# The feed forward's left operands: made by rows and transposed by DMA, with the shift moved into the bias

## The chip, the cores and the metric

The kernel runs on one core of a Trainium2 chip. The metric is the device time of one execution in microseconds (us); lower is better. The engines named below are PE (matmul), PEld (its weight load, which overlaps PE), DVE (vector), ACT (scalar), POOL, and SP, which here only issues DMAs. All DMAs of one core share 16 DMA engines.

## The reference, cut to what matters

The reference is one transformer-like block with modulation (adaLN): a long convolution in place of attention, then a linear layer with a low-rank update in place of the feed forward. The input `x` is 4 x 1024 x 2048 in float32.

```python
mod = (silu(c) @ wmod).reshape(4, 6, 1, -1)
sa, ca, ga, sb, cb, gb = (mod[:, i] for i in range(6))
ga, gb = (sign(g) * max(abs(g), 0.25) for g in (ga, gb))
h = layernorm(x) * (1 + ca) + sa
x = x + ga * (causal_conv(h, K) + D[0] * h)        # K, 2048 taps, comes from the S4 parameters
h = layernorm(x) * (1 + cb) + sb                   # second modulation
out = h @ W.T + bias + sum_e coeffs[e] * scales[e] * (h @ A[e].T) @ Bf[e].T
return x + gb * out
```

The last two lines are the feed forward. The low-rank update is linear in `h`, so the kernel adds it to `W.T` once (it calls the sum the merged weight) and the feed forward is one product of 4096 rows by 2048 by 2048.

## The kernel before

**Convolution part.** 32 row tiles `r` of 128 rows go through `conv_prep` (normalise, transpose by PE, scale and shift, split into two float16 halves), `conv_mm` (a Toeplitz product on PE) and `conv_post` (the result goes to the DRAM array `x1d`, with the statistics for the second layer norm in `ln2`). Between the matmuls of a row tile there are ten ticks; the table `PLAN` says what is emitted in each. "S" is one step of the generator `rest`, which spreads other work over the rows: `prep_lora` (low-rank factors), `section` (one of the six modulation vectors from `wmod`, 16 loads of 1 MB and 64 matmuls each), and `merge`, eight times, which makes the merged weight for two blocks of 128 inner positions, scales each inner position by a power of two (`winv` is the inverse), and writes the weight operands to the DRAM array `wcd`. Every `MR` steps of the merge there is one step of a section. `fold_scale` at the end of `rest` folds `winv` and a common power of two into the modulation's columns `cb` (scale) and `sb` (shift).

**Feed forward part.** The output is cut in 16 units `u` of 256 rows, done twice, for two halves `q` of the columns. Each 256 x 2048 by 2048 x 1024 product is made by Strassen's scheme with seven products instead of eight. Operand `i` of the seven is a 1024 x 128 left tile in two float16 halves (`hl`, "lf" in the profile) and a weight `w` of 1024 x 512 in two halves. `ffn_unit` runs the seven products in the order `ORDER = (0, 4, 5, 1, 6, 2, 3)`, 24 matmuls each (line 750 of the profile), and combines them through `copy` (ACT, line 758) and `finish` (DVE, lines 773 and 774). After each product there is a tick.

**The left operands.** `left` makes the seven left tiles of a unit. It loads the unit's two row tiles from `x1d` and normalises them on ACT (line 690), transposes 16 blocks of 128 columns of both on PE (line 700, tile `tp`, 32 transposes a unit), scales and shifts each block on ACT, because channels now lie on partitions (line 702, tile `gt`), forms sums on DVE (lines 719 to 726), and `put` splits each into halves on ACT and DVE (lines 712 and 713). In the first pass, `q` = 0, these tiles are used straight from SBUF; `put` also writes them to the DRAM array `lfd`. In the second pass, `left_load` reads them back with a plain DMA (line 733). In the first pass the tick of `ffn_unit` emits parts of the next unit's `left` by the table `LPLAN`: four ticks of a unit carry eight PE transposes each. The left tiles of unit 0 are made in the convolution's last two rows.

**Queues.** Nearly all DMAs are issued by SP, in one order: weight loads (line 989), residual loads `xo` (line 767), output stores (line 775), `lfd` stores (line 714), `x1d` loads (line 689). An issue that has to wait holds back those behind it.

Of the kernel before, what the change touches and what calls it, by code (L numbers as in the profile page):

```python
# [12 lines left out]
F32 = mybir.dt.float32  # L13
# [11 lines left out]
P = 128  # L25
# [9 lines left out]
class Net:  # L35
# [302 lines left out]
    def mod_gate(self, pool, name, bias=None):  # L338
# [10 lines left out]
        if bias is not None:  # L349
            bt = pool.tile([P, 512], F32, tag="mg2", name="mg2")  # L350
            for q in range(4):
                nc.sync.dma_start(out=bt[32 * q : 32 * q + 32], in_=bias[ds(512 * q, 512)].partition_broadcast(32))
            v.tensor_tensor(bt, bt, g, MUL)
            outs.append(bt)
# [9 lines left out]
    def fold_scale(self, pool, mul, add, name, winv=None):  # L364
        v = self.nc.vector
        if winv is not None:
            for t in (mul, add):
                v.tensor_tensor(t, t, winv.unsqueeze(2).to_broadcast([P, NC, NB]), MUL)
        b = pool.tile([P, 2, NB], F32, tag="fsb", name="fsb")
        for i, t in enumerate((mul, add)):  # L370
            v.tensor_reduce(b[:, i, :], t.rearrange("p c b -> p b c"), AX.X, ALU.max, apply_absolute_value=True)
        m = pool.tile([P, NB], F32, tag="fsm", name="fsm")
        v.scalar_tensor_tensor(m, b[:, 0, :], LNMAX, b[:, 1, :], MUL, ADD)
        self.hs, inv = s, _ = self.pow2(self.cst, self.allmax(pool, m, NB, name), NB, name)
        for t in (mul, add):
# [91 lines left out]
    def merge(self, pool, tmp, c):  # L467
# [11 lines left out]
        for h in range(2):  # L479
            for q in range(4):  # L480
# [8 lines left out]
                yield  # L489

# [192 lines left out]
    def left(self, pl, u, res):  # L683
        nc, v = self.nc, self.nc.vector
        b = u // 4
        xs = []
# [8 lines left out]
        t = pl["t"].tile([P, NC, 2, P], F32, tag="t", name="gt")  # L695
        for c0 in range(0, NC, 2):
            tp = self.tps.tile([P, 2, 2, P], F32, tag="t", name="tp2")
            for c in range(2):
                for r in range(2):
                    nc.tensor.transpose(tp[:, c, r], xs[r][:, ds(P * (c0 + c), P)], self.ident)  # L700
            for c in range(2):
                nc.scalar.activation(  # L702
                    t[:, c0 + c], tp[:, c], AF.Identity,
                    bias=self.sb[:, c0 + c, b : b + 1], scale=self.cb[:, c0 + c, b : b + 1],
                )
            yield
        a11, a12 = t[:, 0:HC, 0, :], t[:, HC:NC, 0, :]
        a21, a22 = t[:, 0:HC, 1, :], t[:, HC:NC, 1, :]

        def put(i, s):  # L710
            hl = pl["l"].tile([P, HC, 2, P], F16, tag="l", name="lf")
            nc.scalar.copy(hl[:, :, 0, :], s)
            v.tensor_tensor(hl[:, :, 1, :], s, hl[:, :, 0, :], SUB)
            STQ(nc).dma_start(out=self.lfd[u, i], in_=hl)
            res[i] = hl

        put(0, a11)
        s = pl["s"].tile([P, HC, P], F32, tag="s", name="s")
        v.tensor_tensor(s, a21, a22, ADD)
        put(4, s)  # L720
        v.tensor_tensor(s, s, a11, SUB)
        put(5, s)
        put(1, a12)
        v.tensor_tensor(a21, a11, a21, SUB)
        put(6, a21)
        v.tensor_tensor(s, a12, s, SUB)
        put(2, s)
        put(3, a22)
        yield

    def left_load(self, pl, u, i):
        hl = pl["l"].tile([P, HC, 2, P], F16, tag="l", name="lf")
        self.nc.sync.dma_start(out=hl, in_=self.lfd[u, i])
        return hl

    def left_again(self, pl, u):
        return {i: self.left_load(pl, u, i) for i in ORDER}

    def ffn_unit(self, pl, u, q, lf, wc, tick):
# [3 lines left out]
        def prod(i, name):  # L743
# [4 lines left out]
            for k in range(HC):  # L748
                for x, y in ((0, 0), (0, 1), (1, 0)):
                    nc.tensor.matmul(  # L750
                        ps[name], lf[i][:, k, x, :], wc[i][k // 4][:, k % 4, y, :],
# [58 lines left out]
MR = 2  # L810
ACC, TPS = 5, 2
PLAN = ("PNSL", "NL", "NSL", "NTL", "SL", "SL", "SL", "SL", "FSL", "SSL")
LPLAN = ("LL", "LL", "LL", "LL", "L", "0", "")
# [19 lines left out]
def net(ctx: ExitStack, tc: tile.TileContext, io):  # L833
# [6 lines left out]
    k.lfd = k.dram.tile([NU, 7, P, HC, 2, P], F16, tag="lfd", name="lfd")  # L840
# [12 lines left out]
    def section(sec, pools):  # L853
# [5 lines left out]
        if sec == 0:  # L859
            k.sa = k.mod_column(msm, k.kpool, "sa", 0.0)  # L860
            k.hinv = k.fold_scale(msm, k.ca, k.sa, "fs1")
# [4 lines left out]
        elif sec == 4:  # L866
            k.cb = k.mod_column(msm, k.cst, "cb", 1.0)
        elif sec == 3:
            k.sb = k.mod_column(msm, k.cst, "sb", 0.0)
        else:  # L870
            _, k.gbd = k.mod_gate(msm, "gbd", io["bias"])
        yield

    def merges():
        yield from k.prep_lora(pl["lora"], pl["mrg"])
        for c in range(HC):
# [290 lines left out]
```

## Time and profile before

| | |
|---|---|
| time, median of 3 runs | 2144.5 us (2140.22 to 2147.28) |
| time of the profiled execution | 2141.87 us |
| span of the profiled execution | 2140.1 us |
| PE busy | 2082.4 us (97%) |
| DVE, ACT busy | 1308.4 us (61%), 923.7 us (43%) |
| moved by DMA | 484.11 MB, mean 226 GB/s |
| granted clock of PE, mean | 0.988 |

The span runs from the first to the last instruction of the program; the execution's own time is 1.8 us more. "Busy" is the union of an engine's instructions. In rows of groups the line is that of the code, the tile names follow, then the count, the busy time in us and the mean duration of one instruction in ns, then the idle time of the engine just before them and what ended it. The row of PEclk gives the clock granted to PE in tenths of full speed, and the row of DMA the mean busy share of the 16 DMA engines.

### The profile page before, as it was taken

The numbers are of one execution on the slowest core, as the hardware profiler recorded it, in microseconds if no ns is written. First come the engines' busy times: TensorE is split into PE (matmuls) and PEld (weight loads), VectorE is DVE, ScalarE is ACT, GpSimd is POOL, SyncE is SP. The second block draws the span as 40 slices with busy tenths as digits, with TensorE's granted clock in tenths as the row PEclk, the third lists the DMA queues.
The fourth block names the chain that finished last, engine by engine and source line by source line (L and its number), as shares of the span: only waits on it lengthen the run. The fifth ranks groups of instructions, "written<-read, shape, count | busy, mean of one in ns | idle before, by whom it ended". The sixth has DMA issues, their size and how long they took to land.

```text
span 2140.1 us, 28438 instructions
## 1 busy us (share of the span) xinstructions
PE 2082.4 (97%) x11113; PEld 1026.1 (48%) x11113; DVE 1308.4 (61%) x2353; ACT 923.7 (43%) x1695; POOL 6.3 (0%) x18
## 2 busy tenths in 40 slices
PE   7898999999999999999999999999999999999998
PEld 2344455555555555554545545555444444444444
DVE  5439898898979999665565565575533323332323
ACT  1325876677767777745454555555200000000000
POOL 0000000000000000000000000000000000000000
PEclk7999999999999999999999999999999999999999
DMA  9977566787776554387564564564794645454542
GB/s 401 373 307 278 225 227 265 285 310 262 276 278 227 187 192 173 139 346 258 190 241 180 202 240 179 203 235 172 283 341 163 192 151 167 164 170 165 177 157 69
DMA packets 127236, 484.11 MB, mean 226 GB/s; under 512 B 13608, under 2 KB 13768, under 8 KB 95998
## 3 DMA queue, kind: packets, MB, share of 16 engines
q1 hardware_dynamic: 126192, 477.55, 61.4%
q10 hardware_dynamic: 526, 2.63, 0.4%
q8 instruction: 87, 1.43, 0.3%
q0 software_dynamic: 384, 2.11, 0.2%
q14 instruction: 47, 0.39, 0.0%
HBM read 326.94 MB, written 155.30 MB: 225 GB/s over the span
## 4 chain that ended last, share of the span: by engine, by line
PE 67%; DVE 18%; ACT 6%; DMA 5%; issue 2%; SPq 0%; ACTq 0%; POOL 0%; DVEq 0%; POOLq 0%
PE fZ L750 22%; PE fY L750 15%; PE fX L750 15%; PE ya L614 5%; PE yb L614 3%; PE tp L700 3%; DVE wch L514 2%; PE modps L317 2%; DVE st L540 2%; DVE hc L593 2%; DVE y L641 2%; ACT x L660 2%; DMA wcd<-wch 1%; ACT t L582 1%; PE lps L486 1%
## 5 line engine op out<-in xcount | busy, mean ns | idle before, releaser
L750 PEld LDWEIGHTS <-lf 128*128 128x128 f16 x5376 | 526.0, 98 | 620.9 <-issue 1.4
L750 PE MATMUL fZ<-w,lf 128*128 128x512 f16 x2304 | 513.6, 379 | 0.8 <-ACT p L758 0.8
L750 PE MATMUL fX<-w,lf 128*128 128x512 f16 x1536 | 342.8, 379 | 0.0
L750 PE MATMUL fY<-w,lf 128*128 128x512 f16 x1536 | 342.0, 379 | 0.0
L614 PEld LDWEIGHTS <-hc 128*128 128x128 f16 x2304 | 215.3, 98 | 204.6 <-issue 41.6
L768 DVE TENSOR_TENSOR xo<-xo,gb 128x512 f32<-128x512 f32 x128 | 87.8, 690 | 238.7 <-DMA xo<-x1d 227.2
L582 ACT ACTIVATE t<-tp,sa,ca 128x128 f32<-128x128 f32 x480 | 188.1, 471 | 21.6 <-PE tp L578 12.9
L614 PE MATMUL ya<-kh,hs 128*128 128x512 f16 (+3 forms) x768 | 193.7, 326 | 3.7 <-DVE kh L284 2.6
L614 PE MATMUL ya<-kh,hc 128*128 128x512 f16 (+3 forms) x768 | 192.7, 328 | 3.8 <-ACT qs L627 3.6
L614 PE MATMUL yb<-kh,hc 128*128 128x512 f16 (+3 forms) x768 | 192.2, 327 | 1.8 <-DVE y L640 1.4
L758 ACT COPY p<-fZ 128x512 f32<-128x512 f32 x64 | 37.2, 581 | 286.8 <-PE fZ L750 272.1
L614 PEld LDWEIGHTS <-hs 128*128 128x128 f16 x1152 | 105.9, 98 | 108.6 <-issue 28.4
L758 ACT COPY p<-fX 128x512 f32<-128x512 f32 x32 | 18.7, 585 | 316.3 <-PE fX L750 210.4
L702 ACT ACTIVATE gt<-tp,sb,cb 128x256 f32<-128x256 f32 x256 | 124.9, 576 | 60.8 <-PE tp L700 60.8
L317 PE MATMUL modps<-wm,sct 128*32 128x512 f32 x768 | 118.8, 662 | 14.1 <-DMA wm<-in_wmod 14.1
L614 PE MATMUL ya<-kl,hc 128*128 128x512 f16 (+3 forms) x384 | 125.8, 328 | 0.0
L614 PE MATMUL ya<-kl,hs 128*128 128x512 f16 (+3 forms) x384 | 125.1, 326 | 0.7 <-DVE kl L285 0.7
L614 PE MATMUL yb<-kl,hc 128*128 128x512 f16 (+3 forms) x384 | 125.6, 327 | 0.0
L773 DVE TENSOR_TENSOR fin<-fX,gb 128x512 f32<-128x512 f32 x32 | 22.1, 692 | 128.4 <-PE fX L750 128.3
L593 DVE TENSOR_TENSOR hc<-t,hc 128x512 f16<-128x512 f32 x128 | 87.5, 684 | 6.6 <-ACT hc L592 6.4
L486 PE MATMUL lps<-lbh,lac 128*128 128x512 f16 x256 | 86.3, 379 | 1.2 <-DVE we L488 1.2
L578 PE MATMUL tp<-ident,n 128*128 128x128 f32 x512 | 79.3, 280 | 8.1 <-ACT t L582 6.3
(264 smaller groups left out, 2228.0 us busy)
## 6 DMA issues: line engine op xcount, KB each, us to landing
wm<-in_wmod SPq DMA_DIRECT2D x96, 1024.0 KB
lfd<-lf SPq DMA_DIRECT2D x112, 512.0 KB
lf<-lfd SPq DMA_DIRECT2D x112, 512.0 KB
x<-in_x SPq DMA_DIRECT2D x32, 1024.0 KB
x1d<-y SPq DMA_DIRECT2D x32, 1024.0 KB
x<-x1d SPq DMA_DIRECT2D x32, 1024.0 KB
xo<-x1d SPq DMA_DIRECT2D x128, 256.0 KB
out<-xo SPq DMA_DIRECT2D x128, 256.0 KB
```

The source lines that it names most:

```text
L317: self.last = self.nc.tensor.matmul(self.modps[32 * g : 32 * g + 32, :], self.sct[:, j].rearrange("p r b -> p (r b)"), w[:, ds(512 * g, 512)],
L486: nc.tensor.matmul(ps, la[:, x, k, h], y[:, k, osl], start=(n == 0), stop=(n == 5))
L514: v.tensor_tensor(hl[:, :, 1, :], tv, hl[:, :, 0, :], SUB)
L578: nc.tensor.transpose(tp[:, k], n[:, ds(P * (c0 + k), P)], self.ident)
L582: nc.scalar.activation(t[:, k], tp[:, k], AF.Identity, bias=self.sa[:, c, b : b + 1], scale=self.ca[:, c, b : b + 1],)
L593: v.tensor_tensor(lo[:, sl], src, hi[:, sl], SUB)
L614: nc.tensor.matmul(pf[:, o:512], h, self.kf[f][z][:, ds(k0, 512 - o)], start=first, stop=(i == last and (x, z) == (1, 0)), skip_group_chec ...
L700: nc.tensor.transpose(tp[:, c, r], xs[r][:, ds(P * (c0 + c), P)], self.ident)
L702: nc.scalar.activation(t[:, c0 + c], tp[:, c], AF.Identity, bias=self.sb[:, c0 + c, b : b + 1], scale=self.cb[:, c0 + c, b : b + 1],)
L750: nc.tensor.matmul(ps[name], lf[i][:, k, x, :], wc[i][k // 4][:, k % 4, y, :], start=(first and n == 0), stop=(n == 3 * HC - 1), skip_grou ...
L758: nc.scalar.copy(t, ps[name])
L768: v.tensor_tensor(x, x, self.gbias[:, h], ADD)
```

## The change

The left tiles are no longer transposed by PE. `left` scales the two normalised row tiles while they still lie by rows, with a row of scales that is broadcast to all partitions (`cbr`), forms the sums by rows, splits them, and writes them to `lfd` by rows. Both passes then read each operand with a transposing DMA (`dma_start_transpose`), one per product, issued `LAG` = 2 products after the same operand of the unit before was used. The shift `sb` no longer enters the left tiles: `merge` multiplies it with the merged weight (`sbw`), and `mod_gate` adds the result to the bias. So the section of `sb` is computed first, the sections run in the order 3, 4, 5, and the steps of `rest` are paced differently (`MR` = 4, no skipping of every second call in the early rows). The weight loads of the second pass are emitted in the ticks of the last unit of the first pass.

```diff
@@ mod_gate
+            v.tensor_tensor(bt, bt, more, ADD)
             v.tensor_tensor(bt, bt, g, MUL)
@@ merge, after the low-rank update of we
+        ps = self.tps.tile([P, 512], F32, tag="t", name="swp")
+        for h in range(2):
+            for g in range(4):
+                nc.tensor.matmul(
+                    ps[32 * g : 32 * g + 32, :],
+                    self.sbt[:, c + HC * h].rearrange("p r b -> p (r b)"),
+                    we[:, h, ds(512 * g, 512)],
+                    start=(h == 0), stop=(h == 1), skip_group_check=True,
+                )
+        if c == 0:
+            v.tensor_copy(self.sbw, ps)
+        else:
+            v.tensor_tensor(self.sbw, self.sbw, ps, ADD)
+        yield
@@
+    def shift_rows(self, pool, sb):
+        v = self.nc.vector
+        self.sbt = pool.tile([P, NC, 8, NB], F32, tag="sbt", name="sbt")
+        v.tensor_copy(
+            self.sbt.rearrange("p c r b -> p r c b"), sb.unsqueeze(1).to_broadcast([P, 8, NC, NB])
+        )
+        self.sbw = pool.tile([P, 512], F32, tag="sbw", name="sbw")
+
+    def scale_rows(self, pool):
+        nc = self.nc
+        ps = self.tps.tile([NC * NB, P], F32, tag="t", name="cbp")
+        nc.tensor.transpose(ps, self.cb.rearrange("p c b -> p (c b)"), self.ident)
+        row = pool.tile([NC * NB, P], F32, tag="cbr", name="cbr")
+        nc.vector.tensor_copy(row, ps)
+        self.cbd = self.dram.tile([NC, NB, P], F32, tag="cbd", name="cbd")
+        nc.scalar.dma_start(out=self.cbd.rearrange("c b p -> (c b) p"), in_=row)
@@ left
+        if u % 4 == 0:
+            self.cbr = pl["cb"].tile([P, NC, P], F32, tag="cb", name="cbb")
+            nc.sync.dma_start(out=self.cbr, in_=self.cbd[:, b, :].partition_broadcast(P))
@@
-        t = pl["t"].tile([P, NC, 2, P], F32, tag="t", name="gt")
-        for c0 in range(0, NC, 2):
-            tp = self.tps.tile([P, 2, 2, P], F32, tag="t", name="tp2")
-            for c in range(2):
-                for r in range(2):
-                    nc.tensor.transpose(tp[:, c, r], xs[r][:, ds(P * (c0 + c), P)], self.ident)
-            for c in range(2):
-                nc.scalar.activation(
-                    t[:, c0 + c], tp[:, c], AF.Identity,
-                    bias=self.sb[:, c0 + c, b : b + 1], scale=self.cb[:, c0 + c, b : b + 1],
-                )
+        cb = self.cbr.rearrange("p c d -> p (c d)")
+        for x in xs:
+            v.tensor_tensor(x, x, cb, MUL)
             yield
@@
-            hl = pl["l"].tile([P, HC, 2, P], F16, tag="l", name="lf")
-            nc.scalar.copy(hl[:, :, 0, :], s)
-            v.tensor_tensor(hl[:, :, 1, :], s, hl[:, :, 0, :], SUB)
+            hl = pl["nl"].tile([P, 2, 1024], F16, tag="nl", name="nl")
+            nc.scalar.copy(hl[:, 0], s)
+            v.tensor_tensor(hl[:, 1], s, hl[:, 0], SUB)
             STQ(nc).dma_start(out=self.lfd[u, i], in_=hl)
@@ left_load
-        hl = pl["l"].tile([P, HC, 2, P], F16, tag="l", name="lf")
-        self.nc.sync.dma_start(out=hl, in_=self.lfd[u, i])
+        hl = pl["l"].tile([P, 2, HC, P], F16, tag="l", name="lf")
+        self.nc.sync.dma_start_transpose(
+            out=hl.rearrange("p x c r -> p (x c) r"), in_=self.lfd[u, i].rearrange("r x d -> r (x d)")
+        )
@@ tables
-MR = 2
+MR = 4
+LAG = 2
-LPLAN = ("LL", "LL", "LL", "LL", "L", "0", "")
+LPLAN = ("LLL", "L", "L", "L", "L", "LL", "0")
@@ net: the left tiles have 7 buffers (8 before), the row tiles nl have 2
+    def again(n, j):
+        if j < LAG:
+            n, j = n - 1, j + 7
+        i, n = ORDER[j - LAG], n + 1
+        if 0 < n < 2 * NU:
+            lf.setdefault(divmod(n, NU), {})[i] = k.left_load(pr, n % NU, i)
@@ tick of the feed forward
+                k0 = len(done)
+                done.append(k0)
+                if q == 0:
+                    for a in next(plan):
+                        if a == "0":
+                            gens[0] = next_left(u + 2)
+                        take(gens[0], 1)
+                    if u == NU - 1:
+                        load_w(1, ORDER[k0])
+                again(q * NU + u, k0)
```

## Prediction, made before the changed kernel ran

> **What bounds the kernel now.** I read the page's busy row and its 40 slices first, then windows by stage, then PE's timeline in a steady unit.
>
> ```profile
> PE 2082.4 (97%) x11113; PEld 1026.1 (48%) x11113; DVE 1308.4 (61%) x2353; ACT 923.7 (43%) x1695; POOL 6.3 (0%) x18
> ...
> PE   7898999999999999999999999999999999999998
> ...
> PEclk7999999999999999999999999999999999999999
> DMA  9977566787776554387564564564794645454542
> ...
> q1 hardware_dynamic: 126192, 477.55, 61.4%
> ```
>
> PE is busy in nearly every slice at full clock: what leaves PE shortens the kernel, what comes to PE lengthens it. The last row gives the price of plain DMA traffic: 477.55 MB in 61.4% of 2140.1 us is 363 GB/s while the engines work. The windows (two steady units of the first pass, the second pass, the convolution):
>
> ```profile
> core 0: us, PE busy (x) PEld busy (x) DVE busy (x) ACT busy (x) POOL busy (x), PEclk, DMA share, GB/s
> 300.00:500.00 200.00, 195.82 (x1211) 100.40 (x1209) 173.35 (x362) 135.37 (x275) 0.00 (x0) 1.00 0.77 285
> 500.00:700.00 200.00, 198.02 (x1215) 103.04 (x1213) 183.20 (x372) 141.74 (x294) 0.00 (x0) 1.00 0.70 259
> 1065.00:1144.50 79.50, 79.50 (x403) 40.10 (x401) 48.16 (x58) 41.33 (x59) 0.00 (x0) 1.00 0.57 205
> 1640.00:1700.00 60.00, 60.00 (x280) 27.20 (x279) 18.32 (x27) 3.51 (x6) 0.00 (x0) 1.00 0.51 163
> ```
>
> In the feed forward PE never stops, DVE is at 60% in the first pass, and the DMA engines at 57%. In the convolution DVE is near its limit too (183 of 200 us). Now PE's timeline in a unit:
>
> ```profile
> 1075.35 5.34 PE L750 MATMUL fZ<-w,lf 128*128 128x512 f16 x24
> 1080.53 5.34 PE L750 MATMUL fX<-w,lf 128*128 128x512 f16 x24
> 1085.71 1.04 PE L700 MATMUL tp<-ident,x 128*128 128x128 f32 x8
> 1086.58 5.34 PE L750 MATMUL fY<-w,lf 128*128 128x512 f16 x24
> ```
>
> A product follows a product after 5.18 us; with eight transposes between them it follows after 6.05. So a group of eight costs 0.87 us, a unit of seven products 36.26 us bare, and 39.75 with its four groups (the window of 79.50 is two units).
>
> **The change part by part.**
>
> *Transposes removed (L700).* 480 of the 512 lie after 918.9 us, where the feed forward starts: 60 groups x 0.87 = -52.2 us, all on the path. Unit 0's 32 lie between convolution matmuls, where PE is also the limit: 4 x 0.87 = -3.5.
>
> *ACT.* 16 L702 a unit fall away (32 of them, 569 ns each, 15.5 us of busy time in two units); ACT drops from 20.7 to 12.9 us a unit. It was covered by PE, so it is worth nothing.
>
> *DVE, first pass.* Two multiplications of 128x2048 f32 come to each unit. The nearest row is the addition of that shape in the convolution (L414, 2288 ns): +4.6 us on 24.1, so 28.7 of 36.3 us. PE covers it: at most 2.3 us are put ahead of an accumulator's copy, and `acc` has five buffers for three names. If this cover were gone it would cost up to 2 x 2.3 us a unit.
>
> *Shift into the bias.* 64 f32 matmuls (`sbw`) of the shape of L317. In the timeline eight of those hold PE for 1.00 us (513.52 to 514.52 below), so 64 cost +8.0. They also wait for DVE's last piece of the merged weight, and share the two transposing buffers `t` with the convolution. PE's nearest wait of this kind (lps on DVE `we`) was 1.2 us once; from nothing to 1.2 us x 8 = 10, I take 4. DVE gets eight adds from PSUM (743 ns for the nearest row, L488: 6 us), beside PE but on an engine at 92%; they are in that 4. Queued behind PE's wait are convolution matmuls; for them wait the `y` sums on DVE. `scale_rows`, `shift_rows` and the bias add are single instructions, beside PE.
>
> ```profile
> 513.52 1.07 PE L317 MATMUL modps<-wm,sct 128*32 128x512 f32 x8
> 514.52 0.39 PE L614 MATMUL ya<-kh,hs 128*128 128x512 f16 x1
> ```
>
> *Re-pacing of `rest`.* The order 3, 4, 5 and MR = 4 move 48 loads of 1 MB and the 16 weight loads on SP to other ticks. By the yields there are 188 steps instead of 193, so they end at about the same row. DMA had 23 to 30% to spare there: nothing, with 10 us lost or gained as bounds.
>
> *Transposing DMAs.* The 112 plain loads of the second pass (L733) become 224 transposing ones. One serves each 5.18 us product, issued five products, 26 us, ahead of use; latency is hidden unless rate fails. No row shows a transposing DMA. The lower bound on its cost is a plain load of 512 KB: 0.524 MB at 363 GB/s = 1.44 us of all 16 engines. What decides is the first pass, where plain traffic already takes 0.57 x 39.75 = 22.7 us a unit, and 36.26 us are left for everything. Seven loads fit if each takes under (36.26 - 22.7) / 7 = 1.94 us (270 GB/s).
>
> Two rules of the Trainium skill bear on this. "DMA: Bandwidth & Descriptors", section "Latency and other measured facts", puts a transposing DMA at 350 to 400 GB/s where the source is contiguous and 261 measured where it is not. That makes 1.3 to 2.0 us a load: 31.9 to 36.8 us of DMA a unit: well inside PE's 36.26, or 0.5 over. "VectorE: DVE Perf Modes", section "The three transpose paths", speaks against the change: 1309 ns for one 128x128 block by DMA, 390 by PE. Here PE's transposes cost 109 ns each (0.87 / 8), less than its figure, since they are pipelined. If 1309 were a rate, a load of 16 blocks would take 20.9 us, 224 of them 4690 us, and the kernel would run over 5000 us. I read it as the time of one block alone, mostly latency. I take 261 GB/s, the measured one of the page's figures and the nearest to the plain row from below: 0.5 us over PE in 14 units, +7. The rate stays the largest unknown.
>
> *SP's queue.* 24 issues a unit instead of 17; L733 took 320 ns each, so 7.7 us of 36. A load waits for the store of its `lfd` tile, two products earlier, and behind it stand stores of `out` and loads of `xo`, for which DVE waits. If a transposing issue holds SP for 2 or 3 us, 7 x 3 + 17 x 0.32 = 26 us, still under 36.
>
> *First units.* In 930 to 950 us DMA was at its limit (share 1.01 and 1.02), loading the weights. Unit 1's left tiles then came straight from SBUF; now they queue behind the weights, are stored and read back. From 918.9 on 10.5 MB of weights, 3.7 stored, 3.7 read and 3 of the rest are 57 us at 363 GB/s, against 67 us until unit 1's last product starts. From nothing to 15 us of stall, I take +6. At the turn of the passes DMA is full too (1520 to 1580), but the same bytes moved before without a stall: nothing.
>
> *Second pass.* DMA share 0.51, so 18.5 us a unit of which 10.1 were the plain loads; seven at 2.0 us make 22.5 of 36.26. Nothing.
>
> Sum: -52.2 - 3.5 + 8.0 + 4 + 7 + 6 = -30.7. The profiled execution took 2141.9 us (span 2140.1 and 1.8 around it), so 2111.2; the median of the runs shown is 2.6 above that execution, so 2114.
>
> **The rivals.**
>
> *Slower: the transposing loads become the bound of the first pass.* The edge comes early: of the sum, 14 x 3.48 = 48.7 us stand on the steady units, and what is left without them and their +7 is 7 (the transposes of units 0 and 1) - 18 = 11 us of loss. The kernel breaks even when a steady unit takes 39.75 - 11 / 14 = 39.0 us, with a load at (39.0 - 22.7) / 7 = 2.32 us (226 GB/s). At 3 us a unit takes 43.7: +3.95 x 14 + 11 = +66, 2211 us. At 4 us 50.7: +10.95 x 14 + 11 = +164, 2309. Above 3.9 us the second pass follows ((36.26 - 8.4) / 7 = 3.98). For it: no row shows that a transfer which reorders every element runs at a copy's rate, the second rule says it doesn't, and there is a single SP queue in which the transposes stand between all other transfers, at a DMA share of 0.95 or more. Against it: the weight loads ran at 409 to 424 GB/s, so the mixture may have more to give than 363.
>
> *Nothing left: DMA just full.* At 2.25 to 2.4 us a load, all within a few us of 2144.
>
> *The gain is eaten in the convolution.* Steps of `rest` are doubled in rows 3 and 4, and PE's `sbw` matmuls wait for a DVE that is at 92%. For it: DVE 141.84 of 150 us from 700 to 850. Against it: PE waited for others under 10 us in all between 240 and 920 us. It would give 10 to 15 us back: 2126.
>
> *It does not do what it says:* a transposing DMA could be moved element by element. That is the far end of the first rival, several times the time of now.
>
> **How the numbers follow.** Hidden behind PE, 2097 to 2128: 0.42, predicted 2114. Convolution eats part of it, or DMA a little over PE, 2120 to 2137: 0.11. Near no change: 0.05. Slower by the first rival: 0.42, half of it below 2250. 0.3%, some 6.4 us, is about what a measurement of this kernel can tell from no change. Faster is then 0.53, same 0.05, slower 0.42. The likeliest case with its smaller variants has 2097 to 2137 as its own range. The full range begins at 2095 (no stall anywhere: -47.7) and reaches to a load of 3.7 us (48.6 us a unit: +8.85 x 14 + 11 = +135), 2280, leaving out some 0.2 above.
>
> **What the profile would show.** Right: no L700 row with `x`; products 5.18 us apart through the first pass, a unit at 36.3; 64 matmuls `sbw`; DMA share in the first pass at 0.9 to 1.0; no wait of PE on lf; DVE near 28 us a unit. Wrong: PE idle, with DMA lf<-lfd as what ended it, at a regular distance of over 5.2 us between products; or xo<-x1d as DVE's wait growing far over the 227 us of now and `out` stores held on SP; or the first product moved later than 925 us, which would put the loss in the convolution. A DMA share below 0.9 with PE waiting on lf would mean that the issue or the transposing itself, not the bytes, sets the rate.

## The result and the profile after

| | before | after |
|---|---|---|
| time, median | 2145.3 us (2140.22 to 2147.28) | 2256.95 us (2252.22 to 2257.93) |
| ratio after / before | | 1.052, 95% interval 1.0496 to 1.0544 |
| span of the profiled execution | 2140.1 us | 2256.1 us |
| first product of the feed forward starts at | 918.9 us | 942.0 us |
| first pass, 16 units | 635.3 us, 39.7 each | 700.9 us, 43.8 each |
| first unit of the second pass | 36.4 us | 64.0 us |
| later units of the second pass | 36.3 us | 36.3 us |

The kernel is 5.2% slower. The last four rows, read from the timeline of PE (a unit is seven products; it is counted from the end of the unit before, with the idle time ahead of it), give the place of the 116 us of span: 23.1 in the convolution part, 65.6 in the first pass, 27.6 at the turn of the passes. The second pass proper costs nothing. A unit's time in the runs below is the mean of all 16 units of the first pass, where nothing else is said. Of the run e3 only two of four executions are given; the other two were over 1.5% longer, at a slightly lower clock. The page's busy row, the slices and the first queue:

```profile
PE 2078.0 (92%) x10730; PEld 977.1 (43%) x10730; DVE 1385.1 (61%) x2393; ACT 805.5 (36%) x1439; POOL 6.2 (0%) x18
...
PE   6989999999999999997988898798869999999999
...
PEclk8989999999999999998999999999989999999999
DMA  9987857666766648799999999999999787878873
...
DMA packets 585361, 547.03 MB, mean 242 GB/s; under 512 B 477816, under 2 KB 486232, under 8 KB 554126
...
q1 hardware_dynamic: 584240, 540.49, 82.0%
```

PE's row has holes from slice 19 to 30 and none after, and the row of DMA is at 9 over the same slices. There are 458,752 packets of 256 bytes that before did not have: 224 transposing loads of 2048 packets each. Bytes on this queue grew by 13%, its time from 61.4% of a shorter span to 82.0%. Windows (columns: engines, granted clock, DMA share, GB/s) of the first pass, the turn and the second pass:

```profile
985.00:1545.00 560.00, 486.74 (x2131) 213.64 (x2129) 347.35 (x372) 162.01 (x159) 0.00 (x0) 0.94 1.01 267
1640.00:1700.00 60.00, 41.43 (x151) 16.19 (x150) 10.18 (x15) 2.34 (x4) 0.00 (x0) 0.86 1.06 281
1760.00:2120.00 360.00, 360.00 (x1670) 163.23 (x1668) 114.45 (x171) 22.82 (x39) 0.00 (x0) 1.00 0.79 167
```

Before, the first and last of these windows had a DMA share of 0.59 and 0.48 with PE never idle:

```profile
985.00:1545.00 560.00, 560.00 (x2806) 280.74 (x2804) 333.47 (x395) 281.80 (x396) 0.00 (x0) 1.00 0.59 212
1760.00:2120.00 360.00, 360.00 (x1670) 163.18 (x1669) 115.30 (x171) 23.41 (x40) 0.00 (x0) 1.00 0.48 158
```

The price of a transposing load comes out three times. Second pass: the share rose by 0.31 of 36.26 us for seven loads, which is 1.6 us a load more than a plain one (about 1.46 us, from 128 packets of 4 KB at some 183 ns on average over 16 engines): 3.1 us. First pass: 1.01 x 43.8 us of DMA a unit less the 0.59 x 39.7 of before is 20.8 for seven: 3.0 us. Packets: 2048 at 22.5 ns on average (median 18), over 16 engines: 2.9 us. The forecast's sum took 2.0.

The issue and the waits of the whole execution:

```profile
L770 SPq DMA_TRANSPOSE lf<-lfd x224: 1671/2870/9476, 843.8 to 2218.8; - x112
...
DMA to landing us min/median/max: 4.4/5.3/11.6
```

```profile
DVE xo L804 <- DMA xo<-x1d: 234.1, 75, 8.9
...
ACT nl L744 <- DMA lfd<-nl: 196.9, 60, 10.0
ACT x L730 <- DMA x<-x1d: 135.6, 27, 10.8
...
DVE x L737 <- ACT x L730: 111.8, 25, 11.3
```

An issue of a transposing load holds SP for 2.87 us in the median (1.67 at least), where a plain issue takes 0.3 to 0.45 in the median. ACT, which the forecast wrote off, stands 332 us behind DMAs. What PE waits for in a steady unit is then this (its timeline; in brackets the idle time before the product and what ended it):

```profile
1218.52 5.34 PE L786 MATMUL fX<-w,lf 128*128 128x512 f16 x24 [1.09 <-ACT p L794]
1230.76 6.90 PE L786 MATMUL fZ<-w,lf 128*128 128x512 f16 x24 [6.90 <-ACT p L794]
1237.49 5.34 PE L786 MATMUL fY<-w,lf 128*128 128x512 f16 x24
1247.88 6.87 PE L786 MATMUL fZ<-w,lf 128*128 128x512 f16 x24 [5.04 <-ACT p L794]
```

PE waits mostly for ACT's copy of an accumulator, less often for the left tile. That line names the last wait of a chain, not its cause; the experiments take the chain apart.

### The profile page after: what moved, and what is told of

Its sections match the earlier page's. It is cut to its first block, busy times and chain, and to the rows that moved or that the text cites. A ratio compares the mean times of both kernels' runs of the same rounds, so it can differ in the third digit from the quotient of the medians.

```text
span 2256.1 us, 27588 instructions
## 1 busy us (share of the span) xinstructions
PE 2078.0 (92%) x10730; PEld 977.1 (43%) x10730; DVE 1385.1 (61%) x2393; ACT 805.5 (36%) x1439; POOL 6.2 (0%) x18
## 4 chain that ended last, share of the span: by engine, by line
PE 50%; DVE 19%; DMA 17%; ACT 6%; SPq 5%; issue 3%; ACTq 0%; POOL 0%; DVEq 0%; POOLq 0%
PE fZ L786 17%; PE fY L786 10%; PE fX L786 10%; DMA lfd<-nl 5%; SPq L770 4%; PE ya L633 4%; DMA xo<-x1d 3%; PE yb L633 3%; DMA x<-x1d 2%; PE modps L317 2%; DVE wch L533 2%; DVE nl L745 2%; DMA wcd<-wch 2%; DVE y L660 1%; DVE st L559 1%
## 5 line engine op out<-in xcount | busy, mean ns | idle before, releaser
L786 PEld LDWEIGHTS <-lf 128*128 128x128 f16 x5376 | 533.5, 99 | 774.9 <-issue 128.3
L786 PE MATMUL fZ<-w,lf 128*128 128x512 f16 x2304 | 541.5, 394 | 86.7 <-ACT p L794 74.7
L786 PE MATMUL fY<-w,lf 128*128 128x512 f16 x1536 | 347.5, 383 | 14.6 <-DMA lf<-lfd 14.6
L633 PEld LDWEIGHTS <-hc 128*128 128x128 f16 x2304 | 213.8, 98 | 214.0 <-issue 52.2
L737 DVE TENSOR_TENSOR x<-x,cbb 128x2048 f32<-128x2048 f32 x32 | 73.2, 2286 | 111.8 <-ACT x L730 111.8
L794 ACT COPY p<-fZ 128x512 f32<-128x512 f32 x64 | 37.2, 582 | 278.5 <-PE fZ L786 228.4
L730 ACT ACTIVATE x<-x,ln 128x2048 f32<-128x2048 f32 x32 | 67.0, 2094 | 135.7 <-DMA x<-x1d 135.6
L744 ACT CAST nl<-s 128x1024 f16<-128x1024 f32 x48 | 50.2, 1046 | 181.1 <-DMA lfd<-nl 80.1
L744 ACT CAST nl<-x 128x1024 f16<-128x1024 f32 x64 | 66.8, 1043 | 134.1 <-DMA lfd<-nl 116.8
L745 DVE TENSOR_TENSOR nl<-x,nl 128x1024 f16<-128x1024 f32 x64 | 78.2, 1221 | 56.7 <-ACT nl L744 56.7
```

The source lines that it names most:

```text
L633: nc.tensor.matmul(pf[:, o:512], h, self.kf[f][z][:, ds(k0, 512 - o)], start=first, stop=(i == last and (x, z) == (1, 0)), skip_group_chec ...
L730: nc.scalar.activation(x, x, AF.Identity, bias=self.ln2[:, 2 * u + r, 0:1], scale=self.ln2[:, 2 * u + r, 1:2])
L737: v.tensor_tensor(x, x, cb, MUL)
L744: nc.scalar.copy(hl[:, 0], s)
L745: v.tensor_tensor(hl[:, 1], s, hl[:, 0], SUB)
L786: nc.tensor.matmul(ps[name], lf[i][:, x, k, :], wc[i][k // 4][:, k % 4, y, :], start=(first and n == 0), stop=(n == 3 * HC - 1), skip_grou ...
```

## The experiments

The theory after the result: the engines' time for transposing loads bounds the first pass. The rivals: SP's hold by each issue, waits on ACT or DVE, and the convolution. Every run is timed beside before on the same chip; the ratio is to that before.

**e1: the same kernel with plain loads.** All waits, buffers and issues stay; the tiles are read untransposed, as they are in e5 and in e13 to e17, which build on it.

```diff
-        self.nc.sync.dma_start_transpose(
-            out=hl.rearrange("p x c r -> p (x c) r"), in_=self.lfd[u, i].rearrange("r x d -> r (x d)"))
+        self.nc.sync.dma_start(out=hl.rearrange("p x c r -> p x (c r)"), in_=self.lfd[u, i])
```

> The changed kernel with its 224 transposing loads made plain loads of the same 512 KB; nothing is transposed, everything else stays. Theory 1 (a transposing load holds the 16 DMA engines for about 3.06 us: (44.1 - 22.7) / 7 from the steady unit of the first pass): the first pass needs 22.7 + 7 x 1.44 = 32.8 us of DMA a unit, so PE bounds it again at 36.3; the first pass falls from 698 to about 585 us and the stall at the turn of the passes (64 us for a unit instead of 36.3) goes; the convolution keeps its +23. So 942 + 585 + 580 + 7 = 2114 to 2125 us. Theory 2 (the pass is bound by the stores, the row tiles' buffers or DVE's multiplications, not by the transposing): units stay above 40 us, time above 2190.

Measured: 2175.23 us (2171.21 to 2175.87), ratio 1.0151 (1.0136 to 1.0166). The unit takes 40.4 us, the first unit of the second pass 36.6, the first product starts at 937.5. So 82 of the 112 us hang on the transposing, and the whole stall at the turn. But even with loads at a copy's price the kernel loses 33 us: the expectation missed, and with it the thought that one cause explains all. Window and waits of the first pass in e1:

```profile
985.00:1545.00 560.00, 521.27 (x2318) 230.98 (x2317) 384.63 (x411) 181.82 (x178) 0.00 (x0) 0.96 0.86 295
```

```profile
ACT x L730 <- DMA x<-x1d: 116.6, 25, 9.6
ACT nl L744 <- DMA lfd<-nl: 106.3, 49, 6.9
...
PE fZ L784 <- ACT p L792: 38.7, 16, 5.2
```

DMA is not full (0.86) and PE is idle for 39 of 560 us. ACT normalises a row tile in place, so it waits for the `x1d` load; it writes `nl`, which has two buffers, so it waits for the `lfd` store of two operands before. Behind these waits on ACT's queue stand the copies of accumulators, and `fZ` is wanted again by PE two products later.

**e2: four of the seven operands transposing.**

```diff
+        if i in (0, 5, 6, 3):
             self.nc.sync.dma_start_transpose(...
+        else:
+            self.nc.sync.dma_start(out=hl.rearrange("p x c r -> p x (c r)"), in_=self.lfd[u, i])
```

> The changed kernel with four of the seven operands of a unit (0, 5, 6, 3) read by a transposing load and three by a plain load of the same size; those three are left untransposed. Theory 1 (DMA engines' time): a steady unit of the first pass takes 22.7 + 4 x 3.06 + 3 x 1.44 = 39.3 us, so some 14 x 3 = 42 us above the kernel with plain loads alone: 2155 to 2170. Theory 2b (each issue holds SP for 2.87 us in the median and delays what stands behind it): SP is held 4 x 2.87 + 20 x 0.4 = 19.5 us of 36.3 and is no longer late; the time falls to within 15 us of the kernel with plain loads.

Measured: 2222.24 us (2217.38 to 2227.44), ratio 1.0375 (1.0352 to 1.0397); the unit 42.6 us, the turn's unit 53.3. From 0 to 4 to 7 transposing loads the unit goes 40.4, 42.6, 43.8. The time that the engines' theory expected is missed, but it was built on a time for plain loads that e1 missed too. Counted from e1, the run lies 47 us higher; the engines' theory had given 42, the theory of SP's hold at most 15. Between 1060 and 1500 us the DMA share is 1.00, and issues hold SP for 0.63 of the time.

**e3 and e8: other queues.** e3 issues the transposing loads on ACT's queue, e8 moves the `xo` loads and `out` stores to POOL's.

```diff
-        self.nc.sync.dma_start_transpose(            # e3
+        self.nc.scalar.dma_start_transpose(
...
-            nc.sync.dma_start(out=x, in_=at(self.x1d...   # e8, and the store of out alike
+            nc.gpsimd.dma_start(out=x, in_=at(self.x1d...
```

> The changed kernel with all its transposing loads issued by ACT's queue instead of SP's. Theory 1 (DMA engines' time): the same bytes are moved in the same way, so a steady unit stays at 43 to 45 us and the time at 2235 to 2275, or more if ACT, held by the issues, makes its copies late. Theory 2b (SP is held): SP has 17 issues left, stores and residual loads are no longer behind transposes, ACT has 12.9 us of work and 7 x 2.9 us of holds in a unit; the unit falls to 37 to 40 us and the time to 2150 to 2190.

> The changed kernel with the loads of xo and the stores of out issued by POOL's queue, which has nothing else to do then, instead of SP's. Theory 1 (DMA engines' time): 16 engines have the same bytes to move, so units stay near 43 us: 2240 to 2290. Theory 2b (transposes hold SP and make xo and out late, so that DVE and the accumulators wait): 8 of 24 issues leave SP and are late no more; units fall to 38 to 40 us, 2170 to 2205.

Measured: e3 2362.05 and 2367.58 us, ratio 1.104 (1.1018 to 1.1062); e8 2352.1 us (2350.2 to 2358.33), ratio 1.0998 (1.0973 to 1.1022). Units take 51 and 50 us. Neither tells SP from the engines: in e3 the issues now hold ACT, and PE waits 156.3 us for its copies of `fZ`; in e8 POOL is the late one (between 985 and 1545 us it waits 258.8 us for the results that it stores and 244.1 for buffers of `xo`, and DVE waits 211.3 for its `xo` loads). They are failures of design, and show only that SP was the better place.

**e4 and e9: the bias half alone.** e4 is before with `sbw`, the order 3, 4, 5 and `MR` = 4, the transposes left on PE. e9 is e4 without the `sbw` matmuls and their adds, so the shift is left out.

```diff
-        ps = self.tps.tile([P, 512], F32, tag="t", name="swp")     # e9 against e4
-        for h in range(2):
-            for g in range(4):
-                nc.tensor.matmul(ps[32 * g : 32 * g + 32, :], ...
```

> The kernel before with only the second half of the change: the shift goes into the bias (sbw), the sections run in the order 3, 4, 5, MR = 4, no skipped calls; the left operands are transposed by PE as before. Theory A (the convolution's loss of 23 us comes from this half): the trace of the changed kernel has 128 PE records of sbw, two for each f32 matmul in the code, so they hold PE for 16 us and not 8; with a few us of stalls the time is 2144.5 + 16 to 24 = 2160 to 2168, and the feed forward is unchanged. Theory B (the loss comes from unit 0's left operands in rows 30 and 31, where ACT waits for x1d): 16 us of matmuls are hidden in PE's idle time and the time is 2145 to 2152.

> The kernel with the second half of the change alone (2154.7 us, first product at 931.7 us instead of 918.9), with the 64 sbw matmuls and their adds left out: the bias then lacks the shift's part; order and pacing of the steps stay as changed. Theory A (the loss is the matmuls' time on PE, 128 records x 0.125 = 16 us, less a few us of idle time that they fill): time 2138 to 2146, first product at 916 to 921. Rival (the new order and pacing of loads, sections and merges is what costs): 2150 to 2156, first product at 928 or later.

Measured: e4 2154.65 us (2153.64 to 2158.21), ratio 1.0064 (1.0047 to 1.0081), first product at 931.7. e9 2144.25 us (2139.01 to 2151.69), ratio 1.0005 (0.9991 to 1.0019), first product at 922.2. e4 lies between the two times that were expected. The re-pacing is free within the intervals, the matmuls are not: they cost 9.5 us by the first product, and 11.4 by the times, each taken against its own before. Their row in after:

```profile
L498 PE MATMUL swp<-we,sbt x128: 592/592/617, 302.2 to 742.2; 128*32 128x512 f32 x128
```

64 instructions leave 128 records. The forecast read eight records of this shape in 1.00 us as eight instructions; at 0.125 us a record they are 16 us of PE time, not 8.

**e5 and e6: room for ACT.** Three `nl` buffers, `x1d` loaded a step before ACT normalises, `LAG` = 3; e5 with plain loads, e6 with transposing ones.

```diff
...                                # the move of the x1d loads
-LAG = 2
+LAG = 3
-LPLAN = ("LLL", "L", "L", "L", "L", "LL", "0")
+LPLAN = ("", "LLL", "L", "LL", "L", "LL", "0")
-        ..., ("nl", 2), ...
+        ..., ("nl", 3), ...
```

> The kernel with plain loads (nothing transposed) took 2175 us, with units of 40.3 us in the first pass, though its DMA share was 0.86: PE waited 43 us for ACT's copy of fZ, because ACT stood behind stores of nl (two buffers, 106 us of waits) and x1d loads (117 us). Here the same kernel, still with plain loads, gets three nl buffers instead of two, the x1d loads a step ahead of their normalisation, and LAG 3 with LPLAN ("", LLL, L, LL, L, LL, 0). Theory 1 (ACT's waits hold back the copies, since Z is used three times in a unit with one product between): units fall to 36.3 to 37.5 us, PE <- ACT p below 15 us, time 2112 to 2135. Rival (DVE with its multiplications, or DMA at 0.86, sets the unit of 40 us): 2165 to 2180.

> The same three edits on the changed kernel, with all loads transposing. Theory 1 (DMA engines' time is the bound once ACT is cured): plain traffic and plain loads need 0.86 x 40.3 = 34.7 us a unit, transposing adds (0.775 - 0.53) x 36.26 = 8.9 us by the second passes' DMA shares, together 43.6, which is what the changed kernel has (698 / 16): the time stays at 2235 to 2260. Rival (ACT's waits are the first cause, and transposing only makes them longer): units fall to 38 to 40 us, time 2170 to 2205.

Measured: e5 2153.45 us (2149.58 to 2158.29), ratio 1.0065 (1.004 to 1.009); e6 2237.92 us (2235.62 to 2239.9), ratio 1.0462 (1.0438 to 1.0486). In e5 the unit falls from 40.4 to 38.7 us: ACT's waits were real and cost about 2 us of the 4 that e1's unit lies above the bare 36.3. The cure was expected to give 36.3 to 37.5 us, so something else is left, and no run names it. In e6 the unit falls only from 43.8 to 42.4. e6 lies 84 us above e5: with ACT given room, the transposing costs as much as between e1 and after. Window and PE's waits of e6:

```profile
985.00:1530.00 545.00, 484.06 (x2147) 212.00 (x2146) 346.63 (x375) 162.83 (x161) 0.00 (x0) 0.97 1.05 277
```

```profile
PE fX L786 <- DMA lf<-lfd: 32.4, 15, 6.2
PE fZ L786 <- DMA lf<-lfd: 29.1, 14, 4.9
PE fZ L786 <- ACT p L794: 21.7, 8, 6.3
```

ACT's wait went from 74.7 to 21.7 us, and the wait on the left tiles took its place (30 to 66). At a DMA share of 1.05 moving waits won little.

**e7: the second pass with every load issued twice.** The second pass has no ACT chain and no stores of left tiles.

```diff
             lf.setdefault(divmod(n, NU), {})[i] = k.left_load(pr, n % NU, i)
+            if n > NU:
+                k.left_twice(pr, n % NU, i)      # the same load into a spare tile
```

> The changed kernel, with every transposing load of the second pass but those of its first unit issued a second time into an unused tile. It measures the price by itself, where ACT and DVE have little to do. Theory 1 (a load holds the 16 DMA engines for 2.7 us): xo and out need 0.53 x 36.26 - 7 x 1.44 = 9.1 us a unit, 14 loads 38, together 47 us: some 15 x 10.8 = 160 us more, 2400 to 2430. Theory 2b (the least hold of SP, 1.67 us, is the rate): 14 x 1.67 + 8 x 0.4 = 27 us a unit, hidden behind PE's 36.3: 2250 to 2270.

Measured: 2408.19 us (2405 to 2411.38), ratio 1.1255 (1.1219 to 1.129); the eleven units from 1734 to 2289 us take 50.4 us on average. The window of its second pass, with these units in it:

```profile
1720.00:2294.00 574.00, 445.99 (x1940) 195.21 (x1939) 134.19 (x202) 24.52 (x45) 0.00 (x0) 0.88 1.08 216
```

The engines are full, at 1.08 (1.00 up to 2400 us). That is 620 us, in which 184 transposing loads were issued. With the other traffic at 9.1 us a unit, 104 in all, they took (620 - 104) / 184 = 2.8 us each. Issues held SP for 0.92 of this window, 2.6 us a transposing load, so this run prices the load and doesn't tell the two apart.

**e10, e11 and e12: e6 with one thing removed each.** e10 leaves out the stores of `out` in the first pass, e11 the second pass's weight loads, and e12 cuts ACT's and DVE's work on the left operands loose from the DMAs (they work on tiles that no transfer fills or reads; the transfers stay). One line of e12's edit is printed; it also leaves one `nl` buffer and lets ACT and DVE work in turn on a single tile.

```diff
-            STQ(nc).dma_start(out=at(self.io["out"]...      # e10: only if q == 1
...
-                    if u == NU - 1:                          # e11
-                        load_w(1, ORDER[k0])
...
-            STQ(nc).dma_start(out=self.lfd[u, i], in_=hl)    # e12
+            STQ(nc).dma_start(out=self.lfd[u, i], in_=self.fix)
```

> The kernel with three nl buffers, early x1d loads and LAG 3, all loads transposing (2237.9 us, 42.3 us a unit in the first pass, DMA share 1.05), with the stores of out left out in the first pass, so half of the output is not written. They are 1.05 MB a unit, 2.9 us of 16 engines at 363 GB/s. Theory 1 (the first pass is bound by the DMA engines' time): the unit falls by 2 to 3 us to 39.3 to 40.3, the time to 2190 to 2206. Rival (a chain of store, landing, transposing load sets the unit, or the SP queue's 2.9 us holds, with engines busy only because packets wait): taking stores away that nothing waits for but the xo buffers changes the unit by under 1 us, 2222 to 2240.

> The same kernel (2237.9 us, first unit of the second pass 61.1 us), with the reload of the weights for the second pass left out: the second pass then multiplies with the first pass's weights. Theory (at the turn 14.7 MB of weights, some 38 us, meet 7 transposing loads of 3.04 us and 5.8 us of xo and out in each of two units: 38 + 2 x 27.1 = 92 us against 72.5 us of PE): without the weights the first unit of the second pass takes 36.3 to 38 us, the time is 2208 to 2216. Rival (the stall comes from SP's order or from the last left tiles being late): the unit stays above 50 us, 2228 or more.

> The kernel with early x1d loads and LAG 3, all loads transposing (2237.9 us, 42.3 us a unit in the first pass), with the chain through ACT and DVE cut from the DMAs: the stores to lfd come from a tile that is never rewritten, the x1d loads go to tiles that nobody reads, and ACT and DVE do the same instructions on a tile of their own. The left operands' values are therefore not the right ones; bytes, transposing loads and busy times are the same. Theory D (the transposing loads' rate, at the DMA engines or at SP's issue, holds the first pass by itself): PE waits on lf, units stay at 41 to 43 us, 2215 to 2240. Theory C (ACT's waits for landings hold it, through the copies): units fall to 36.3 to 38 us, 2140 to 2175.

Measured: e10 2209.45 us (2204.05 to 2218.49), ratio 1.0313 (1.0287 to 1.034); e11 2212.77 us (2204.55 to 2219.42), ratio 1.0315 (1.0285 to 1.0345); e12 2224.93 us (2221.95 to 2226.23), ratio 1.0385 (1.0368 to 1.0403).

In e10 the unit hardly changes, 42.2 us after 42.4. The engines' theory wanted 2 to 3 us less, so this miss speaks against the engines' time as the only limit. The time falls all the same, in the profile mostly at the turn (60.9 to 52.9 us) and ahead of the first product (5 us). PE's waits on left tiles nearly vanish and those on ACT return:

```profile
PE fZ L786 <- ACT p L794: 64.9, 17, 8.6
PE fX L786 <- DMA lf<-lfd: 6.7, 3, 2.9
```

So two limits lie close together, and each takes over when the other is eased. e12 was to tell whether the DMA side is enough by itself. With the chain cut, the unit is still 42.6 us. Its window, PE's two longest waits, and DVE's longest in this window:

```profile
1060.00:1560.00 500.00, 442.71 (x1959) 195.76 (x1958) 322.55 (x347) 148.27 (x145) 0.00 (x0) 0.94 1.02 259
...
PE fZ L786 <- ACT p L794: 70.9, 15, 10.1
PE fZ L786 <- DMA lf<-lfd: 9.1, 2, 5.3
...
DVE xo L804 <- DMA xo<-x1d: 95.3, 42, 6.2
```

PE still waits for ACT's copies here, hardly for left tiles. ACT waits for DVE, with which it now shares a tile, and DVE waits for `xo` loads. A DMA that comes late still reaches PE by way of DVE, and the edit has added a chain of its own, so e12 does not decide. In e11 the first unit of the second pass falls from 60.9 to 36.3 us, and in e1 it was 36.6: the stall at the turn needs both the 14.7 MB of second weights and the transposing loads.

**e13 to e17: SP's hold or the engines' time?** All are e5 with something added behind each load of the first pass: small DMAs of 256 bytes on SP (eight in e13, four in e15, six and four in e16 and e17, where they are tied to the load before them), which hold SP and move next to nothing; or in e14 one plain copy of 512 KB within DRAM, which takes the engines' time and one issue.

```diff
             lf.setdefault(divmod(n, NU), {})[i] = k.left_load(pr, n % NU, i)
+            for _ in range(HOLD):                              # e13, e15; e16, e17 in
+                nc.sync.dma_start(out=k.scr[held[0]], in_=k.ident[0:16, 0:4])   # issue_after(load)
+            nc.sync.dma_start(out=k.scr[held[0]], in_=k.lfd[n, i]...)           # e14
```

> The kernel with plain loads, three nl buffers and early x1d loads (2153.5 us, 38.5 us a unit), with eight DMAs of 256 bytes put behind each load of the first pass on SP's queue. They move next to nothing, but eight issues at 0.32 us and more hold SP as a transposing load does (2.65 to 3.9 us in the traces). Theory 2b (SP's holds make stores and loads late): units rise to 41 to 43 us, 2195 to 2230. Theory 1 (the DMA engines' time): 38.5 to 39.5 us, 2150 to 2170.

> The same kernel with plain loads (2153.5 us, 38.5 us a unit, DMA share 0.89), with one plain DMA of 512 KB from DRAM to DRAM behind each load of the first pass: 7 x 1.45 = 10 us more of the DMA engines' time in a unit, which is what transposing adds (7 x (2.88 - 1.46) by the packets' mean times), with a single issue of some 0.4 us on SP. Theory 1 (the DMA engines' time): units rise to 42 to 45 us, 2205 to 2255. Theory 2b (SP's holds): 38.5 to 40 us, 2150 to 2175.

> The kernel of e13 with four small DMAs behind each load instead of eight. In e13 an issue took 0.70 us, so eight held SP for 5.6 us, more than any transposing load (3.9 us on average in the first pass), and the units rose to 47 us on average. Four hold it for 2.8 us, 3.4 with the load itself, which is nearly the size in question. Theory 2b (SP's hold at the size it has in the changed kernel is enough to cost 4 us a unit): 41 to 43 us, 2195 to 2225. Theory 1 (the engines' time is what costs, SP's hold follows from it): 38.5 to 39.5 us, 2150 to 2172.

> This is e5 (plain loads, three nl buffers, x1d loads a step ahead) with six small DMAs of 256 bytes issued on SP directly behind each of the first pass's loads; unlike in e15 they are tied to the load before them, so that they stay at that place in SP's order. At 0.42 us an issue (the median in e15) they hold SP for 2.5 us more, with 0.38 of the load itself 2.9 us, which is the hold of a transposing load (2.8 us median in e6), while they give the DMA engines next to nothing to move. If SP's hold alone costs what e6 lost against e5, the unit goes from 38.5 to 41 to 43 us and the time to 2195 to 2225. If the engines' time decides and SP's hold is free at this size, the unit stays at 38.5 to 39.5 us and the time at 2150 to 2172.

> e16 with four small DMAs behind each load instead of six. In e16 one small issue held SP for 0.61 us on average and the load itself for 0.58, so a load and its six held it for 4.2 us; a load and four should hold it for 3.0 us, close to the 2.8 us median (3.9 mean) of a transposing load in e6. e16 gave 46.6 us a unit with a DMA share of only 0.78, so 8.1 us over e5 with SP's hold 3.6 us longer a load. If the loss grows in proportion with the hold, this unit takes 43.5 to 45 us, the time is 2225 to 2250, and SP's hold by itself is as large a cause as the engines' time. If the queue only decides above a point that a transposing load does not reach, the unit stays under 40.5 us and the time under 2185.

DMA share and the share of time in which issues held SP (the sum of their own durations) are those of a stretch of the first pass (1060 to 1500 us, e14 to 1540); e5 and e6 stand below for comparison:

| | time, us | ratio (interval) | unit, us | DMA share | SP held |
|---|---|---|---|---|---|
| e13 | 2295.86 (2292.08 to 2298.83) | 1.0716 (1.0697 to 1.0736) | 47.4 | 0.75 | 0.55 |
| e14 | 2235.49 (2234.46 to 2236.91) | 1.0436 (1.042 to 1.0452) | 44.0 | 0.92 | 0.37 |
| e15 | 2157.29 (2152.41 to 2158.71) | 1.0074 (1.0044 to 1.0103) | 39.1 | 0.88 | 0.29 |
| e16 | 2270.16 (2268.89 to 2278.09) | 1.0616 (1.059 to 1.0642) | 45.8 | 0.78 | 0.70 |
| e17 | 2217.57 (2215.78 to 2219.64) | 1.0353 (1.0335 to 1.037) | 42.9 | 0.82 | 0.57 |
| e5 | 2153.45 | 1.0065 | 38.7 | 0.89 | 0.25 |
| e6 | 2237.92 | 1.0462 | 42.4 | 1.05 | 0.84 |

In e14, with issues holding SP for 0.37 of the time, extra work of the DMA engines makes PE wait 98.6 us for left tiles and costs as much as the transposing.

```profile
PE fX L784 <- DMA lf<-lfd: 63.3, 21, 10.5
PE fZ L784 <- DMA lf<-lfd: 26.7, 23, 3.2
PE fY L784 <- DMA lf<-lfd: 8.6, 9, 1.9
```

e13 and e15 failed: the scheduling had moved their small DMAs (in e13 353 of 840 lie before 900 us and 448 after 1240; in e15 only 27 of 420 lie between 1060 and 1520). e16 and e17 delivered them, and both came out on the side that gives the queue weight: 42.9 us a unit in e17, with engines at 0.82 of their time. But neither they nor e14 isolate what they were to test. In the traces the DMAs of SP's queue use eight semaphores in turn, so an issue waits until the DMA eight issues before has landed; every DMA that is added takes one of these places. SP's own waits between 1060 and 1500 us show it, here two lines of e17 and three of e14:

```profile
SPq L801 <- DMA x<-x1d: 34.5, 17, 2.8
SPq L770 <- DMA lf<-lfd: 15.8, 15, 2.4
```

```profile
SPq L770 <- DMA x<-x1d: 15.1, 7, 2.2
SPq L1059 <- DMA x<-x1d: 14.8, 7, 2.1
SPq L729 <- DMA scr<-lfd: 13.3, 10, 2.1
```

All waits of SP on landings sum to 78.8 us of these 440 in e17, 95.9 in e16 and 115.2 in e14, for the most part on transfers that have nothing to do with the tile at hand. In e6 and in after they are 20.6 and 39.3 us, all before a left tile's load and on the store of a left tile. So these three runs slow the kernel in part by a path that takes far less of the time in the change.

What is shown is that the transposing of the loads costs some 80 us (e1 against after, e5 against e6), and that with it the DMA share is 1.00 or more over a stretch of the first pass in after, e2, e6, e10 and e12, where plain loads leave it at 0.86 (e1) and 0.89 (e5). Which of the two sets the pace, the engines' time or SP's hold (0.77 of the time in after, 0.84 in e6), stays open. e2 leans to the engines: SP was held less there than in after, and the loss was still three times what the theory of the hold allowed.

No version here beats before: with ACT given room and the transposing taken away altogether, e5 is still 0.65% above it.

## Why the prediction was wrong, step by step

It forecast 2114 us and faster; 2257 was measured, inside the range. What decided was its own first rival.

- **Transposing loads, 2.0 us each, +7: the step that failed.** A load takes 2.8 to 3.1 us of the engines, above the break-even of 2.32 that the forecast worked out, and plain loads in its place give back some 80 of the 112 us. Its working for 3 us gave a unit of 43.7 us, and 43.8 was measured. That close agreement is in part luck: the same sum leaves plain loads hidden behind PE's 36.3 us, and e1 measured 40.4. The 2211 us of that working are 46 too few, for the most part because of the convolution (23.1 instead of 8.5) and the turn (27.6 instead of nothing). The number 2.0 came from the 261 GB/s in the Trainium skill ("DMA: Bandwidth & Descriptors", section "Latency and other measured facts"); 0.524 MB in 2.9 to 3.0 us is 175 to 181 GB/s here, and the measurement decides. That page has a rule that fits better, in "Why small descriptors are slow": a small descriptor pays a fixed part, 27% at 256 bytes. No run shows whether a packet of a transposing load is such a descriptor, and the loss in the trace is larger: 22.5 ns a packet is 11.4 GB/s an engine, against 22.4 for packets of 4 KB at 183 ns.
- **Transposes on PE, -52.2: right, but not cashed in.** The L700 row is gone and products follow each other after 5.2 us where nothing waits. Units of 43.8 us leave nothing of it.
- **ACT "worth nothing", `acc` covers DVE: wrong.** ACT's busy time fell as said, but between 930 and 1560 us it waits 176.1 us for `lfd` stores, which it hadn't done, and 117.0 for `x1d` loads, against 21.7 before. Five buffers for three names do not cover it; the likely reason is that `fZ` comes three times in a unit with one product between. In e1 the unit lies 4.1 us above the bare one, and e5 got 1.7 of it back.
- **Shift into the bias, 8 + 4 = +12: right in the sum.** e4 gives +12.8 by the first product and +12.2 by the times. That the sum fits is luck, since the parts were wrong: the matmuls are 16 us of PE, not 8, and cost 9.5 to 11.4 us, so part of them seems to fill PE's idle time; and PE's waits for DVE ahead of the first product, which were to add up to 4, went from 3.3 to 3.8 us in e4.
- **Unit 0, -3.5: wrong.** Made by rows, it moves the first product by +5.8 (e1 against e4), and its transposing loads by +4.5 (after against e1), where it was to save 3.5. The DMA queue and the DVE that the convolution already uses are the likely reason, not a tested one. Together with the bias half this is the 23.1.
- **First units, +6: not seen.** The first two take 43.1 and 37.2 us, no more than the later ones.
- **Turn of the passes, nothing: wrong by 27.6.** "The same bytes moved before without a stall" counted bytes, not time; the loads among them had doubled in price (e1 and e11).
- **Second pass, nothing: right**, at a share of 0.79 instead of the 0.62 worked out (22.5 of 36.26 us).
- **SP's queue: left open** (see e2 and e14 to e17). The hold of 2 to 3 us was foreseen; e3 and e8 show that other queues are no way out here.

## What to carry to other kernels

Price a transfer that reorders elements by its packets, not by its bytes: count them, take the time of one from a trace, and put the sum against the engines' free time in each stage, also where two streams meet for a short while. A run that adds DMAs to load one resource loads the queue's semaphores too: look at the issuing engine's waits before reading it. Before an engine is called covered, list which waits are added to it and what stands behind them: ACT had less work and was later. When two limits lie within 2 us of each other, removing one shows the other, so a pair of runs with one and both removed says more than either alone.

## What the runs showed of the hardware

- A packet of 256 bytes of a transposing DMA takes 18 ns in the median and 22.5 on average, one of 4 KB some 183 ns on average: a sixteenth of the bytes for an eighth of the time.
- The issue of a transposing DMA holds its queue for at least 1.67 us. The mean is 3.7 us between 1060 and 1500 us of after and 2.7 in its second pass, but only 2.6 in e7's second pass, where the engines are full too; what lengthens it stays open.
- A long pause makes the next product slower. In the first pass and at the turn of after:

```profile
1184.80 5.34 PE L786 MATMUL fZ<-w,lf 128*128 128x512 f16 x24 [3.01 <-ACT p L794]
...
1644.30 5.35 PE L786 MATMUL fX<-w,lf 128*128 128x512 f16 x24 [1.36 <-DMA lf<-lfd]
1654.25 6.79 PE L786 MATMUL fY<-w,lf 128*128 128x512 f16 x24 [4.60 <-DMA lf<-lfd]
1663.49 7.04 PE L786 MATMUL fZ<-w,lf 128*128 128x512 f16 x24 [2.45 <-DMA lf<-lfd]
```

In after, products follow pauses of 1.1 to 2.3 us at 5.34 us as ever, and pauses of 3.2 us or more at 6.7 to 8.3. Between 2.4 and 3.0 us both happen. The granted clock of the turn's window was 0.86. The effect is not small: up to the end of the turn PE took 148 us longer than its bare 36.26 us a unit, of which 107 were idle time and 41 slower products. The forecast had no term for it.
